# Softplus' sums on TensorE, rows copied out of PSUM at once, the norm in finer steps, the gate's product on GpSimd

## The chip, the cores and the metric

The kernel runs on one core of a Trainium2 chip. The metric is the device time of one execution in microseconds (us). The core has five engines that run side by side, each through its own list of instructions, in order: TensorE (PE in the profile, its weight loads PEld), VectorE (DVE), ScalarE (ACT), GpSimd (POOL) and SyncE (SP), which here only issues DMAs. They wait for each other through semaphores. SBUF is the working memory; PSUM, eight banks of 128 x 512 fp32 values, takes TensorE's results.

## The reference

The program is a network of four layers on an image of 2 x 256 x 32 x 32. The change lies in layer 0: a group norm, and then two Mamba blocks one after the other, each followed by a layer norm and a residual add. A block, for each of 2 x 1024 tokens with 256 channels and 512 inner channels:

```
xs, res = split(x @ in_w + in_b)
xs = silu(conv4(xs) + conv_b)               # causal, depthwise, 4 taps
dt, B, C = split(xs @ xproj_w)              # 16, 16, 16
delta = softplus(dt @ dt_w + dt_b)
h_t = exp(delta_t * A) * h_(t-1) + delta_t * B_t * xs_t     # 16 states for each channel
y = sum over states of h_t * C_t, + xs * D
out = (y * silu(res)) @ out_w + out_b
x = x + layernorm(out)
```

Layer 1 is a convolution attention over 7 x 7 taps, layers 2 and 3 are attentions with mixtures of experts. The reference computes in fp32.

## The kernel before

**Chunks and slots.** Layer 0 treats its 2048 tokens in chunks of 512. Two blocks of four chunks make eight units, numbered 0 to 7, and their scans follow each other. A tile holds 128 inner channels by 512 tokens, and there are four (dc = 0 to 3). `scan` (L415 on) runs over 16 states n and in each over the four tiles: 64 slots. A slot holds one Exp on ScalarE into PSUM (`m_da`, L468; three banks), one scan on VectorE (`m_h`, L472), one step of the readout of the previous state, and one step of whatever else is paced beside the scan. The right side of the scan, du times B, is made by GpSimd for two tiles at a time (L461), into six buffers, so three states. The readout (`rest`) has four steps for each state: four transposes by TensorE into a bank (`m_ht`, L440; three banks), and a multiply-add by VectorE into `m_ya` (L449), in states 0 and 10 a product by ScalarE.

**What is paced beside it.** `paced` (L552) hands out the steps of several generators over a range of slots. During the scan of a unit these are: `back` of the unit before (gate, product, output projection, norm, residual); `front` of the unit after (input projection, convolution, dt, softplus); weight loads; and `aside`, which folds the weights of layer 1's convolution into taps. The first 9 steps (`GATED`) of `back` lie in slots 0 to 35, its other 7 in slots 40 to 61; the first 22 steps (`HEAD`) of `front` in slots 0 to 38, its other 16, which are softplus', in slots 38 to 62; `aside` in slots 40 to 63. Projections, sums and tap transposes share two banks, `ps_mm`.

**Softplus** is max(z, 0) + log(1 + exp(-|z|)), with a correction for what is lost in rounding 1 + e. ScalarE leaves max(z, 0) in `delta`, exp(-|z|) in `e` and its logarithm in `ln` (the Exp and Ln of four tiles are one instruction each). Then w = (1 + e) - 1 is made, and GpSimd computes e - w (L405), adds it to `ln` (L407), adds that to `delta` (L409), and multiplies delta by `xs` into `du` (L411). The front of unit 0 runs ahead of all scans, with nothing beside it (`alone`), and there VectorE does this work.

**back.** The gate is projected and put through Silu; `m_y` gathers skip and readout by matmuls in a bank, and VectorE multiplies it by the gate (L516). Four output projections go into two banks and stay there; `norm_rows` takes mean and variance of all four from PSUM by VectorE, and ScalarE writes the normalised rows to SBUF (L168). After transposes (L179) and ScalarE's scale and bias (L540), GpSimd adds the result to x, in the second block also the input that is loaded again (L543, L548). The back of unit 7 runs after the last scan, interleaved by `both` with the convolution of image 0 (`early_acc`, 56 steps): one step of `back` after each three of its own.

**Order.** The order on each engine is that in which the built program lists its instructions. It follows the steps above, but the scheduler of the build moves instructions off their places in the source, so the built lists of both kernels were compared, engine by engine.

Of the kernel before, what the change touches and what calls it, by code (L numbers as in the profile page):

```python
# [10 lines left out]
F32 = mybir.dt.float32  # L11
# [8 lines left out]
P = 128  # L20
# [4 lines left out]
C = 256  # L25
# [208 lines left out]
class Mamba:  # L234
# [1 line left out]


    ASIDE = 10
    GATED = 9
    HEAD = 22  # L240

    def __init__(self, net, m, pools, xt, x, in_w, out_w, xproj_w, dt_w):
# [50 lines left out]
    def front(self, j, alone=False):  # L293
# [104 lines left out]
        for dc in range(NDC):  # L398
            w = du[:, dc, :]
            if alone:  # L400
                nc.vector.tensor_scalar(w, e[:, dc, :], 1.0, -1.0, ALU.add, ALU.add)
            else:
                nc.scalar.activation(w, e[:, dc, :], AF.Identity, bias=net.one)
                nc.scalar.activation(w, w, AF.Identity, bias=net.minus_one)
            eng.tensor_sub(w, e[:, dc, :], w)  # L405
            yield
            eng.tensor_add(ln[:, dc, :], ln[:, dc, :], w)  # L407
            yield
            eng.tensor_add(delta[:, dc, :], delta[:, dc, :], ln[:, dc, :])  # L409
            yield  # L410
            eng.tensor_mul(w, delta[:, dc, :], xs[:, dc, :])  # L411
            yield
        self.chunks[j] = xs, bd, ct, delta, du

# [67 lines left out]
            pass  # L482
        return before

    def back(self, j):

        net, nc, m, xt = self.net, self.net.nc, self.m, self.xt
        y, *sums = self.chunks.pop(j)
        tok = slice(j * TC, (j + 1) * TC)
        gate = self.one.tile([P, NDC, TC], F32, tag="gate", name=f"{m}_gate_{j}")  # L490
        for dc in range(NDC):
            ps = self.ps_mm.tile([P, TC], F32, tag="mm", name=f"{m}_g_{j}_{dc}")
            for kc in range(NCC):
                nc.tensor.matmul(
                    ps, lhsT=self.gate_sb[:, kc, dc * P : (dc + 1) * P], rhs=xt[:, kc, tok],
                    start=(kc == 0), stop=(kc == NCC - 1),
                )
            nc.scalar.activation(  # L498
                gate[:, dc, :], ps, AF.Identity, bias=net.col(f"{m}_in_b", NDC + dc)
            )  # L500
            yield
        nc.scalar.activation(gate, gate, AF.Silu)
        yield

        for dc in range(NDC):
            ps = self.ps_mm.tile([P, TC], F32, tag="mm", name=f"{m}_y_{j}_{dc}")
            nc.tensor.matmul(
                ps, lhsT=self.skip[:, dc, :], rhs=y[:, dc, :], start=True, stop=False
            )
            for k, ya in enumerate(sums):  # L510
                for i in range(TPC):
                    nc.tensor.matmul(
                        ps[:, i * P : (i + 1) * P], lhsT=ya[:, i, dc * P : (dc + 1) * P],
                        rhs=net.ident, start=False, stop=(k == 1 and i == TPC - 1),
                    )
            nc.vector.tensor_mul(y[:, dc, :], ps, gate[:, dc, :])  # L516
            yield
        o = self.one.tile([P, TPC, C], F32, tag="o", name=f"{m}_o_{j}")
        found = []
        for i in range(TPC):  # L520
            if i % 2 == 0:
                ps = self.ps_mm.tile([P, TC], F32, tag="mm", name=f"{m}_out_{j}_{i}")
            a = ps[:, i % 2 * C : (i % 2 + 1) * C]
            nc.tensor.matmul(
                a, lhsT=net.ones_row, rhs=self.out_b, start=True, stop=False
            )
            for dc in range(NDC):
                nc.tensor.matmul(  # L528
                    a, lhsT=y[:, dc, i * P : (i + 1) * P], rhs=self.out_sb[:, dc, :],
                    start=False, stop=(dc == NDC - 1),  # L530
                )
            found.append(a)
            yield
        tiles = [o[:, i, :] for i in range(TPC)]
        net.norm_rows(tiles, found, nc.scalar)
        yield
        for cc in range(NCC):
            ps = net.transposed(self.ps_mm, tiles, cc, "mm")
            r = self.one.tile([P, TC], F32, tag="r", name=f"{m}_r_{j}_{cc}", bufs=3)
            nc.scalar.activation(  # L540
                r, ps, AF.Identity, scale=net.col(f"{m}_ln_w", cc), bias=net.col(f"{m}_ln_b", cc)
            )
            nc.gpsimd.tensor_add(xt[:, cc, tok], xt[:, cc, tok], r)  # L543
            if self.x is not None:
                x = self.one.tile([P, TC], F32, tag="r", name=f"{m}_x_{j}_{cc}", bufs=3)
                at = j % (HW // TC) * TC
                nc.sync.dma_start(x, self.x[j // (HW // TC), cc, :, at : at + TC])
                nc.gpsimd.tensor_add(xt[:, cc, tok], xt[:, cc, tok], x)  # L548
            yield
# [25 lines left out]
def layer0(net, x, x_dram, m1, m2, load_image, taps, conv_dram, lg):  # L575
# [5 lines left out]
    with (  # L581
# [32 lines left out]
        for u, (m, j) in enumerate(units):  # L614
# [9 lines left out]
            rest = m.load_rest() if u and j == 0 else iter(())  # L624
            steps += [(f, Mamba.HEAD, 0, 38) for f in fronts]
            steps += [(rest, 1, 37, 38)]
            steps += [(f, 16, 38, 62) for f in fronts] + [(b, 7, 40, 61) for b in done]
            steps += [(rest, 1, 62, 63)]
            if u + 1 < len(units):
                n = 9 if u else 12  # L630
# [18 lines left out]
                acc = {0: taps.bank(ps_acc.tile([P, TC], F32, tag="acc", name="early_acc"))}  # L649
                steps += [(taps.convolve(0, pair, acc), 56, 3, 63)]  # L650
            before = m.scan(j, before, paced(63, steps), u == 0)
            done = [m.back(j)]
        taps.read(acc, lg)
        for _ in before:
            pass
# [1087 lines left out]
```

## Time and profile before

| | us |
|---|---|
| median of three runs | 2186.85 |
| range of the runs | 2185.29 to 2189.43 |
| profiled execution, its own time | 2188.29 |
| span of its profile | 2186.6 |
| busy: TensorE, its weight loads | 1894.0, 1335.5 |
| busy: VectorE, GpSimd, ScalarE | 1400.3, 1028.9, 959.2 |
| first scan, last scan's end | 53.26, 1031.3 |
| convolution of image 0 in the tail | 1034.6 to 1110.2 |

The span runs from the first instruction to the last; the profiled execution's time is 1.7 us longer. A line of the profile names the source line (L472), the engine, the operation and the tiles as `out<-in`; a count, busy us and mean ns of one follow, and then for how long the engine sat idle before such instructions and who released it. TensorE's counts are passes: a matmul of fp32 data is listed as two, a transpose as one. A busy TensorE is not TensorE at its peak, since a pass is listed from its start to its end and passes overlap. Line numbers up to L397 are the same in both kernels.

### The profile page before, as it was taken

The page shows a single profiled execution, that of the slowest core. Times are in us where ns is not written, and L with a number is a line of the kernel's source. Part 1 is how long each engine was busy: PE and PEld are TensorE (multiplying, and loading weights), DVE is VectorE, ACT ScalarE, POOL GpSimd, SP SyncE. Part 2 cuts the span into 40 slices and gives each one's busy share as a digit, 9 for nine tenths or more (in the row PEclk, how much of TensorE's full clock was granted, in tenths as well). Part 3 has the DMA queues.
Part 4 walks back from the last instruction along what each step waited for, and adds up shares of the span by engine and source line. Part 5 has one row for each costly group of instructions (what it writes and reads, how often), then busy time and mean ns, then how long its engine had stood idle before and what let it go on. Part 6 is the DMA issues. An engine that isn't in the chain of part 4 may idle for free.

```text
span 2186.6 us, 27311 instructions
## 1 busy us (share of the span) xinstructions
PE 1894.0 (87%) x9652; PEld 1335.5 (61%) x9652; DVE 1400.3 (64%) x2210; ACT 959.2 (44%) x1610; POOL 1028.9 (47%) x726
## 2 busy tenths in 40 slices
PE   6888898898978888788999989949999599859996
PEld 2464555556555655454646556539999467649995
DVE  6999998999999999899005475752222544432223
ACT  4676677767777767645013454411111132301111
POOL 3796787959698686965025420012332000023331
PEclk9869889898989889899999999969999799979997
DMA  2121121111212111310030100028998200059997
GB/s 106 45 68 39 37 69 35 58 35 45 62 47 60 38 49 35 85 42 17 0 64 1 48 15 10 20 82 306 326 329 323 82 10 10 20 206 327 329 323 292
DMA packets 90499, 223.87 MB, mean 102 GB/s; under 512 B 35467, under 2 KB 51728, under 8 KB 79732
## 3 DMA queue, kind: packets, MB, share of 16 engines
q1 hardware_dynamic: 77636, 198.29, 27.1%
q0 software_dynamic: 7728, 19.15, 2.9%
q10 hardware_dynamic: 4992, 4.59, 0.7%
q8 instruction: 81, 1.33, 0.3%
q14 instruction: 62, 0.51, 0.1%
HBM read 204.60 MB, written 19.37 MB: 102 GB/s over the span
## 4 chain that ended last, share of the span: by engine, by line
PE 32%; DVE 22%; issue 19%; POOL 11%; ACT 10%; DMA 5%; POOLq 0%; SPq 0%; DVEq 0%; ACTq 0%
DVE m_h L472 11%; DVE m_ya L449 6%; PE acc L762 3%; POOL x L1520 3%; POOL l_yd L1570 3%; PE m_ht L440 3%; PE early_acc L762 3%; PE av L1276 3%; ACT m_da L468 2%; PE sc L1250 2%; DMA l_yd<-y,target 2%; POOL m_h L461 2%; PE h L1099 2%; PE m_xd_ps L351 1%; PE w L1108 1%
## 5 line engine op out<-in xcount | busy, mean ns | idle before, releaser
L461 POOL TENSOR_TENSOR m_h<-m_du,m_b 128x1024 f32<-128x1024 f32 x254 | 594.5, 2364 | 196.0 <-PE m_ht L440 95.8
L440 PE MATMUL m_ht<-ident,m_h 128*128 128x128 f32 x2048 | 361.2, 305 | 119.4 <-DVE m_ya L449 83.9
L440 PEld LDWEIGHTS m_ht<-ident,m_h 128*128 128x128 f32 x2048 | 259.5, 154 | 317.8 <-DVE m_ya L449 112.7
L468 ACT ACTIVATE m_da<-m_delta,m_aneg 128x512 f32<-128x512 f32 x512 | 349.5, 690 | 220.8 <-DVE m_h L472 220.1
L1520 POOL DMA_INDIRECT x<-l_zd,source x82 | 84.8, 1034 | 573.1 <-DVE source L1465 217.1
L449 DVE SCALAR_TENSOR_TENSOR m_ya<-m_ht,m_ct,m_ya 128x512 f32<-128x512 f32 x448 | 320.2, 733 | 18.4 <-PE m_ht L440 17.5
L472 DVE TENSOR_TENSOR_SCAN m_h<-m_da,m_state,m_h 128x512 f32<-128x512 f32 x256 | 318.7, 1271 | 14.7 <-POOL m_h L461 8.7
L472 DVE TENSOR_TENSOR_SCAN m_h<-m_da,m_h 128x512 f32<-128x512 f32 x256 | 303.3, 1210 | 23.6 <-ACT m_da L468 13.1
L1550 PEld LDWEIGHTS h<-xts,we 128*128 128x128 f32 x2528 | 298.4, 194 | 7.1 <-issue 3.4
L1550 PE MATMUL h<-xts,we 128*128 128x128 f32 x2528 | 299.4, 277 | 2.2 <-issue 1.7
L1557 DVE TENSOR_TENSOR hid<-hid,h 128x512 f32<-128x512 f32 x79 | 54.3, 688 | 258.9 <-PE h L1550 258.9
L1556 ACT ACTIVATE hid<-h 128x512 f32<-128x512 f32 x79 | 47.2, 598 | 384.6 <-issue 324.0
L1564 PE MATMUL o<-we,hid 128*128 128x256 f32 x632 | 150.4, 380 | 2.2 <-DVE y L1569 1.6
L1570 POOL DMA_INDIRECT l_yd<-y,target x79 | 79.3, 1003 | 142.6 <-DVE y L1569 136.3
L1564 PEld LDWEIGHTS o<-we,hid 128*128 128x128 f32 x632 | 113.7, 190 | 15.7 <-DVE y L1569 2.8
L336 PE MATMUL m_conv<-m_pre,m_taps 128*128 128x512 f32 x240 | 114.6, 596 | 6.7 <-ACT m_gate L498 5.6
L762 PE MATMUL early_acc<-x,early 128*98 128x448 f32 (+21 forms) x308 | 97.0, 447 | 0.0
L762 PE MATMUL acc<-x,pair 128*98 128x416 f32 (+21 forms) x308 | 93.6, 452 | 0.0
L1569 DVE COPY y<-o 128x256 f32<-128x256 f32 x79 | 33.6, 425 | 69.6 <-PE o L1564 69.6
L309 PE MATMUL m_in<-x,m_in_sb 128*128 128x512 f32 x128 | 68.8, 663 | 9.8 <-ACT m_pre L313 6.9
L762 PEld LDWEIGHTS acc<-x,pair 128*98 128x98 f32 x308 | 47.7, 167 | 39.9 <-issue 34.5
L528 PE MATMUL m_out<-m_out_sb,m_xs 128*128 128x256 f32 x256 | 68.7, 397 | 0.0
(318 smaller groups left out, 2843.3 us busy)
## 6 DMA issues: line engine op xcount, KB each, us to landing
we<-in_l_experts_dram SPq DMA_DIRECT2D x82, 1536.0 KB
m_b<-m_bd SPq DMA_DIRECT2D x128, 256.0 KB
w<-in_l_w_dram SPq DMA_DIRECT2D x21, 256.0 KB
l_zd<-l_z SPq DMA_DIRECT2D x7, 512.0 KB
l_yl<-l_yd SPq DMA_DIRECT2D x10, 256.0 KB
l_yl<-l_yd ACTq DMA_DIRECT2D x10, 256.0 KB
early<-taps SPq DMA_DIRECT2D x7, 343.0 KB
pair<-taps SPq DMA_DIRECT2D x7, 343.0 KB
```

Source lines behind the costliest of these rows:

```text
L309: nc.tensor.matmul(ps, lhsT=self.in_sb[:, kc, mc * P : (mc + 1) * P], rhs=self.xt[:, kc, tok], start=(kc == 0), stop=(kc == NCC - 1),)
L336: nc.tensor.matmul(ps, lhsT=self.taps[:, dc * 4 + k, :], rhs=pre[:, dc, k : k + TC], start=(k == 0), stop=(k == 3),)
L440: nc.tensor.transpose(ps[:, dc * P : (dc + 1) * P], hs[dc // G][:, dc % G, i * P : (i + 1) * P], net.ident,)
L449: nc.vector.scalar_tensor_tensor(ya[:, i, :], ps, c, ya[:, i, :], ALU.mult, ALU.add)
L461: (nc.vector if start and n == 0 else nc.gpsimd).tensor_mul(h, du[:, g * G : (g + 1) * G, :], b.unsqueeze(1).to_broadcast(half))
L468: nc.scalar.activation(da, delta[:, dc, :], AF.Exp, scale=self.aneg[:, i : i + 1])
L472: nc.vector.tensor_tensor_scan(h, da, h, 0.0 if first else state[:, n, dc : dc + 1], ALU.mult, ALU.add)
L762: nc.tensor.matmul(a[:, lo - 16 * k : hi - 16 * k, co : co + n], lhsT=lhsT, rhs=self.x[:, kc, b, lo - r0 : hi - r0, ci : ci + n], start=(u ...
L1520: nc.gpsimd.indirect_dma_start(out=x, out_offset=None, in_=zd[:, :], in_offset=bass.IndirectOffsetOnAxis(ap=source[:, g : g + 1], axis=0), ...
L1550: nc.tensor.matmul(ps[:, at], lhsT=w12[:, s, kc, at], rhs=xt[:, kc * P : (kc + 1) * P], start=(kc == 0), stop=(kc == NCC - 1),)
L1564: nc.tensor.matmul(ps[:, :C], lhsT=ht[:, mc * P : (mc + 1) * P], rhs=w[:, 8 + mc, :], start=(mc == 0), stop=(mc == NHC - 1),)
L1570: nc.gpsimd.indirect_dma_start(out=yd[g], out_offset=bass.IndirectOffsetOnAxis(ap=target[:, g : g + 1], axis=0), in_=y, in_offset=None, bo ...
```

## The change

Softplus' e - w and the two adds leave GpSimd. ScalarE now makes w = 1 - (1 + e), TensorE adds delta + e + ln + w in a bank by four matmuls with the identity, ScalarE copies the sum to `delta`, and GpSimd keeps the product with `xs`. In the front of unit 0 (`alone`) VectorE still makes e - w, TensorE adds three terms, and VectorE multiplies straight from PSUM. Softplus takes 12 steps in place of 16, paced over slots 38 to 54.

In `back`, except for unit 7's, ScalarE copies `m_y` out of PSUM and GpSimd multiplies it by the gate, a tile later; the step for the last product makes `GATED` 10. ScalarE copies each pair of output projections to SBUF at once; statistics are taken from SBUF, row tile by row tile, in the following steps, and the normalising is split in two. That makes 10 steps after the gated ones in place of 7, paced over slots 38 to 62 in place of 40 to 61.

```diff
-    GATED = 9
+    GATED = 10
...
             if alone:
                 nc.vector.tensor_scalar(w, e[:, dc, :], 1.0, -1.0, ALU.add, ALU.add)
+                nc.vector.tensor_sub(w, e[:, dc, :], w)
             else:
                 nc.scalar.activation(w, e[:, dc, :], AF.Identity, bias=net.one)
-                nc.scalar.activation(w, w, AF.Identity, bias=net.minus_one)
-            eng.tensor_sub(w, e[:, dc, :], w)
-            yield
-            eng.tensor_add(ln[:, dc, :], ln[:, dc, :], w)
-            yield
-            eng.tensor_add(delta[:, dc, :], delta[:, dc, :], ln[:, dc, :])
-            yield
-            eng.tensor_mul(w, delta[:, dc, :], xs[:, dc, :])
+                nc.scalar.activation(w, w, AF.Identity, scale=-1.0, bias=net.one)
+            yield
+
+            pool, tag = (self.ps_ht, "ht") if alone and dc % 2 else (self.ps_mm, "mm")
+            ps = pool.tile([P, TC], F32, tag=tag, name=f"{m}_sp_{j}_{dc}")
+            parts = (delta, ln, du) if alone else (delta, e, ln, du)
+            for k, a in enumerate(parts):
+                nc.tensor.matmul(
+                    ps, lhsT=net.ident, rhs=a[:, dc, :], start=(k == 0), stop=(k == len(parts) - 1)
+                )
+            nc.scalar.copy(delta[:, dc, :], ps)
+            yield
+            eng.tensor_mul(w, ps if alone else delta[:, dc, :], xs[:, dc, :])
             yield
...
-            nc.vector.tensor_mul(y[:, dc, :], ps, gate[:, dc, :])
-            yield
+            if alone:
+                nc.vector.tensor_mul(y[:, dc, :], ps, gate[:, dc, :])
+            else:
+                nc.scalar.copy(y[:, dc, :], ps)
+                if dc:
+                    nc.gpsimd.tensor_mul(y[:, dc - 1, :], y[:, dc - 1, :], gate[:, dc - 1, :])
+            yield
+        if not alone:
+            nc.gpsimd.tensor_mul(y[:, dc, :], y[:, dc, :], gate[:, dc, :])
+        yield
         o = self.one.tile([P, TPC, C], F32, tag="o", name=f"{m}_o_{j}")
...
-            found.append(a)
-            yield
-        tiles = [o[:, i, :] for i in range(TPC)]
-        net.norm_rows(tiles, found, nc.scalar)
+
+            if i % 2:
+                nc.scalar.copy(
+                    o[:, i - 1 : i + 1, :], ps.rearrange("p (i c) -> p i c", c=C)
+                )
+            if i > 1:
+                stats(i - 2)
+            yield
+        stats(2)
         yield
+        stats(3)
+        rs = net.small.tile([P, TPC], F32, tag="ln_rs", name="ln_rs")
+        net.rstd(rs, mv[:, :, 1])
+        off = net.small.tile([P, TPC], F32, tag="ln_off", name="ln_off")
+        nc.vector.scalar_tensor_tensor(off, mv[:, :, 0], -1.0, rs, ALU.mult, ALU.mult)
+        yield
+        for i, a in enumerate(tiles):
+            nc.scalar.activation(
+                a, a, AF.Identity, scale=rs[:, i : i + 1], bias=off[:, i : i + 1]
+            )
+            if i % 2:
+                yield
...
-            steps += [(f, 16, 38, 62) for f in fronts] + [(b, 7, 40, 61) for b in done]
+            steps += [(f, 12, 38, 54) for f in fronts] + [(b, 10, 38, 62) for b in done]
...
-            done = [m.back(j)]
+            done = [m.back(j, u + 1 == len(units))]
```

More of the change, by code (lines that the diff above doesn't have):

```diff
@@ L483, in scan, with back @@
         return before
-    def back(self, j):
+    def back(self, j, alone=False):
         net, nc, m, xt = self.net, self.net.nc, self.m, self.xt
@@ L515, in back, with stats @@
                     )
-            nc.vector.tensor_mul(y[:, dc, :], ps, gate[:, dc, :])
+            if alone:
[4 more added lines that the diff above has]
+                    nc.gpsimd.tensor_mul(y[:, dc - 1, :], y[:, dc - 1, :], gate[:, dc - 1, :])
             yield
+        if not alone:
+            nc.gpsimd.tensor_mul(y[:, dc, :], y[:, dc, :], gate[:, dc, :])
+        yield
         o = self.one.tile([P, TPC, C], F32, tag="o", name=f"{m}_o_{j}")
-        found = []
+        tiles = [o[:, i, :] for i in range(TPC)]
+        mv = net.small.tile([P, TPC, 2], F32, tag="ln_mv", name="ln_mv")
+        def stats(i):
+            st = net.small.tile([P, 6], F32, tag="ln_st", name="ln_st")
+            nc.vector.bn_stats(out=st, in_=tiles[i])
+            nc.vector.bn_aggr(out=mv[:, i, :], in_=st)
         for i in range(TPC):
```

## The prediction

> **What bounds the kernel now.** I first read the share of each engine in every stretch of 100 us (columns: stretch, its length, busy us of PE, PEld, DVE, ACT, POOL, then TensorE's clock, DMA share, GB/s). The change lies in the stage from 53 to 1117 us.
>
> ```profile
> 400.00:500.00 100.00, 92.11 (x425) 59.46 (x425) 93.96 (x104) 70.15 (x107) 72.74 (x39) 0.88 0.14 45
> 600.00:700.00 100.00, 84.66 (x411) 55.61 (x410) 95.06 (x111) 76.08 (x128) 88.12 (x53) 0.91 0.18 55
> 1000.00:1100.00 100.00, 95.31 (x412) 56.77 (x413) 40.97 (x68) 27.73 (x40) 18.19 (x15) 1.00 0.04 10
> ```
>
> VectorE, busy 91 to 96 us in each 100, sets the pace of the scans; in the tail after them it is TensorE. Next, who VectorE waited for from 50 to 1035 us (total, times, longest):
>
> ```profile
> DVE m_h L472 <- POOL m_h L461: 19.2, 13, 4.9
> DVE m_h L472 <- ACT m_da L468: 19.0, 23, 2.5
> DVE m_ya L449 <- PE m_ht L440: 17.5, 26, 2.2
> DVE m_xs L516 <- PE m_y L512: 1.9, 3, 1.3
> ```
>
> Its idle time there, 57.6 us, is the most that better timing can return. Three groups that the change touches, from 100 to 1000 us (count, busy us, mean ns, idle time before):
>
> ```profile
> L409 POOL TENSOR_TENSOR m_delta<-m_delta,m_ln 128x512 f32<-128x512 f32 x28 | 35.6, 1271 | 1.5
> ...
> L516 DVE TENSOR_TENSOR m_xs<-m_y,m_gate 128x512 f32<-128x512 f32 x28 | 18.9, 674 | 1.9 <-PE m_y L512 1.9
> ...
> L702 ACT COPY w1ts<-w1t 128x512 f32<-128x512 f32 x21 | 12.3, 584 | 4.5 <-PE w1t L700 4.1 <-ACT m_state L432 0.2
> ```
>
> The scans begin a chunk at 543.22, 664.37, 789.13 us, so a chunk takes some 124 us and one of its 64 slots 1.95. I cut chunk 5 at its slots 0, 16, 32, 40, 48, 56 and 64 (same columns):
>
> ```profile
> 722.00:742.00 20.00, 19.53 (x85) 13.50 (x84) 17.96 (x22) 12.55 (x18) 11.26 (x6) 0.74 0.13 28
> 742.00:757.20 15.20, 13.58 (x85) 10.93 (x84) 14.19 (x18) 14.70 (x21) 15.04 (x9) 1.00 0.26 69
> 757.20:771.40 14.20, 8.21 (x38) 5.31 (x36) 14.20 (x20) 8.92 (x14) 14.04 (x9) 0.78 0.05 18
> 771.40:789.10 17.70, 15.16 (x77) 12.07 (x78) 15.61 (x20) 12.07 (x22) 17.39 (x14) 0.70 0.13 35
> ```
>
> From slot 40 on GpSimd is never idle (46.47 of 47.1 us): twelve softplus sums fall there, and the scans wait for its products at the chunk's end. TensorE has 10 us of idle time in it, 6 of them in slots 48 to 56, at a low clock.
>
> **The Trainium skill.** *GPSIMD Engine Reference*, section 1, gives GpSimd no access to PSUM: hence the new copies by ScalarE ahead of the gate's product. *VectorE: DVE Perf Modes*, section "The TRN2 errata", gives a ScalarE read from PSUM (172+N)/1.2 ns, for N = 512 an estimate of 570; the trace has 584, which I use. *TensorE: Matmul & The Clock Gate*, "Architectural detail", says that ScalarE, VectorE and GpSimd are strictly first in, first out, so a waiting copy holds all behind it; agreeing, ScalarE's Exp stands behind each eviction. Its Part 1 lets the clock fall when the array has been idle: four transposes take 0.66 us in the busy stretch at 757.50, 1.11 in the sparse one at 767.04.
>
> **The change, part by part**, against the profiled execution's 2188.29 us (span 2186.6, 1.7 around it). The runs' median is 1.44 lower, so I take the same difference from 2186.85.
>
> 1. *Gate's product.* Seven of eight chunks lose four VectorE products. The mean is 674 ns; from start to start (480.49 to 481.07) one holds VectorE about 0.60: 28 x 0.60 = -17 us on the bounding engine. The statistics now read SBUF: 416 ns on `t` in SBUF, 418 on `m_out` in PSUM, so nothing. ScalarE gets 28 copies of 584 ns, 16 us, covered by its 25 to 30% idle time; without cover, as much again. GpSimd gets 28 products of 1.27, 2.5 us per pair, in slots 18 to 36, where it idles (16.84 of 33 us busy in slots 16 to 32, by the same answer).
>
> 2. *Softplus.* GpSimd loses 84 operations (sub and two adds, 1.18 to 1.27 us): 104 us, 14.9 a chunk, all from slots 38 to 62. Priced from the built order with the rows' durations, it falls from 98 to 88 us a chunk with the four gate products, and that order leaves 5 to 8 us of GpSimd work in every four slots there (before: 10 to 12), against VectorE's 7.4. The 19.2 us wait should nearly go: -17 us. It was at the end of the chunk; what is late next there is TensorE.
>
> 3. *Softplus on TensorE.* Each of 28 tiles takes four matmuls of 128x512, two passes each. Passes follow each other after 0.43 us (four from 547.42 to 549.13): 4 x 2 x 0.43 = 3.44 us, 13.8 a chunk. Pricing the changed order in this way (transpose 0.11, projection step 0.43), TensorE has 31.9 us of work in slots 40 to 58, where VectorE has 30.8 (scan 1.19, `ya` 0.65 from start to start). Until now it had about 17. So it just fits, without its waits. What covers it: the order puts VectorE's `ya` later there, some 7 us behind the transposes that feed them. Without cover, 13.8 - 7 = 7 us a chunk.
>
> 4. *Copies and waits.* ScalarE gets 28 copies of `delta` and 14 of the projections, 584 ns: 25 us. The copy waits for the four matmuls; behind it on ScalarE stands the next Exp, for which a scan waits. The matmuls wait for ScalarE's two Identity steps; behind them on TensorE stand transposes, and behind these GpSimd, which needs the `h` buffers freed. The two `mm` banks alternate among sums, projections and tap transposes, each needing the eviction of the one before the last. Following chunk 5 step by step from slot 36: Exp and Ln with their table loads keep ScalarE 16.9 us between two stretches of Exp (slots 36 to 43: VectorE 16.0, a lead of three scans), 2 us of wait, as before roughly 1; from the first sum to the first scan of n = 11, 1.5 us; the products of n = 13 wait for the second sum, 1 to 2 us. So 2 us a chunk more than the same slots lose today: +14 us. Bounds: 0 (a denser, faster TensorE absorbs it, and holding banks for a shorter time pays) and +7 a chunk (step 3).
>
> 5. *Start.* From Ln (43.34 us) to the first scan (53.26) VectorE does all the sums. They go to TensorE, 3 x 0.86 = 2.6 us a tile, waiting from 43.3: tile 1 is ready at 48.5, tile 2 at 51.1. The product of h takes 1.22, the first scan can start at about 51.8: -1.5 us (0 to -3).
>
> 6. *Tail.* The last back has 20 steps instead of 16, the convolution beside it 56 steps at 3 each: 18 fit. The built order accordingly puts the last 8 transposes behind the convolution's last matmul, formerly 28 matmuls ahead. Before, this came at its end:
>
> ```profile
> 1105.02 1.27 POOL L548 TENSOR_TENSOR x<-x,m_x 128x512 f32<-128x512 f32 x1
> ...
> 1110.26 0.68 POOL L737 MEMSET pair<- 128x686 f32 x1 [2.59 <-PE early_acc L762]
> ```
>
> The second convolution (`acc`) began at 1116.57, 6.4 us after the first ended at 1110.2. Now: transposes 0.5, `r` 0.78, four GpSimd adds of 1.27 with the second x load (held by the first add's buffer) and memsets to about 8.5, then 4.5 pairs of `xs` copies and transposes at 0.9: 12.7 us, less the 0.9 us of transposes no longer inside: +5 us. Bounds +2 to +8. Other loads on SP keep their place apart from a few tap loads among the `b` loads; none ended a long wait before.
>
> Sum: -17 - 17 + 14 - 1.5 + 5 = -16.5 us, hence 2170.
>
> **Rivals.** *TensorE becomes the bound.* Place: slots 40 to 58 of seven chunks; price 7 us each. For: the work nearly doubles there, and TensorE is idle for only 0.5 us in the 20 before slot 40. Against: its low clock and the late `ya`. Then -17 - 17 + 49 - 1.5 + 5 = +18.5: 2205. It decides from (16.5 + 14) / 7 = 4.4 us of new waiting a chunk. *Everything new is hidden*, and early-freed banks take half of the 17.5 us for which VectorE waited on transposes: -17 - 19 - 9 + 2 - 1.5 + 5 = -40: 2147. *The cover was worthless*: GpSimd's products wait for later transposes instead, the 17 us do not return, the rest holds: 2187.
>
> **Chances.** Forecast 0.50, everything hidden 0.18, TensorE the bound 0.21, GpSimd's wait only replaced 0.11. No more than 0.2% (4.4 us) can be told from no change. Faster: 0.48 of the forecast, 0.18, and 0.03 of the last, 0.69. Slower: 0.20 and 0.02, 0.22. The rest, 0.09, is same. The likeliest case alone spans 2158 to 2182 (new waits of 0.3 to 3.7 us a chunk); the range reaches to the centres of the two outer rivals, leaving out half of each: 2145 to 2204.
>
> **What would show it.** Step 1: no gate product on VectorE, its busy time about 17 us lower. Step 2: `m_h` waiting for POOL below 5 us; POOL about 69 us less busy. Steps 3 and 4: TensorE busy above 90% in slots 40 to 58 at a clock near 1, and VectorE's waits for `m_da` and `m_ht` up by 14 us together; above 31 us the prediction falls. Chunks of 120 to 121 us. Step 5: first scan near 51.8. Step 6: `acc` about 11 to 12 us behind the last `early_acc`.

## The result

The changed kernel takes 2199.46 us (median of five runs, 2195.33 to 2200.05); the kernel before, run beside it five times, takes 2185.29. The ratio is 1.0059 with a 95% interval of 1.0045 to 1.0072: slower by 10 to 16 us, where 16.5 us less were forecast. The profiled execution has a span of 2198.3 us, 11.7 more than before. That span is the sum to explain.

### The profile page after: what moved, and what is told of

The parts are those of the page before. It is cut to its first block, busy times and chain, and to the rows that moved or that the text cites. A ratio compares the mean times of both kernels' runs of the same rounds, so it can differ in the third digit from the quotient of the medians.

```text
span 2198.3 us, 27827 instructions
## 1 busy us (share of the span) xinstructions
PE 1958.4 (89%) x9900; PEld 1359.3 (62%) x9900; DVE 1380.7 (63%) x2174; ACT 996.2 (45%) x1686; POOL 959.0 (44%) x670
## 4 chain that ended last, share of the span: by engine, by line
PE 24%; issue 14%; DVE 8%; POOL 8%; DMA 4%; ACT 2%; POOLq 0%; ACTq 0%; DVEq 0%
POOL x L1558 3%; PE acc L800 3%; POOL l_yd L1608 3%; PE av L1314 3%; PE sc L1288 2%; PE early_acc L800 2%; DMA l_yd<-y,target 2%; PE h L1137 2%; DVE m_h L478 2%; DVE m_ya L455 2%; PE w L1146 1%; DMA x<-l_zd,source 1%; POOL band L937 1%; PE l_g L1359 1%; DMA l_yl<-l_yd 1%
## 5 line engine op out<-in xcount | busy, mean ns | idle before, releaser
L446 PEld LDWEIGHTS m_ht<-ident,m_h 128*128 128x128 f32 x2048 | 251.1, 150 | 265.3 <-issue 105.9
L446 PE MATMUL m_ht<-ident,m_h 128*128 128x128 f32 x2048 | 330.0, 293 | 72.4 <-DVE m_ya L455 48.6
L549 PE MATMUL m_out<-m_out_sb,m_xs 128*128 128x256 f32 x256 | 73.1, 428 | 0.0
```

Of the source, the lines that this page charges most:

```text
L446: nc.tensor.transpose(ps[:, dc * P : (dc + 1) * P], hs[dc // G][:, dc % G, i * P : (i + 1) * P], net.ident,)
L549: nc.tensor.matmul(a, lhsT=y[:, dc, i * P : (i + 1) * P], rhs=self.out_sb[:, dc, :], start=False, stop=(dc == NDC - 1),)
```

## The profile after

The shares of the engines in the same three stretches of 100 us as before (columns: stretch, its length, busy us of PE, PEld, DVE, ACT, POOL, TensorE's clock, DMA share, GB/s):

```profile
400.00:500.00 100.00, 90.21 (x431) 54.93 (x430) 92.29 (x103) 72.87 (x111) 71.64 (x37) 0.94 0.16 47
600.00:700.00 100.00, 94.03 (x430) 59.34 (x429) 89.09 (x104) 74.50 (x132) 73.08 (x40) 0.91 0.21 56
1000.00:1100.00 100.00, 93.92 (x412) 56.49 (x410) 46.02 (x63) 30.14 (x43) 23.57 (x12) 1.00 0.01 4
```

TensorE is now as busy as VectorE, from 600 to 700 us more so. Over the whole span VectorE is busy for 1380.7 us (19.6 less), GpSimd for 959.0 (69.9 less). The work left the engines as it was meant to.

Who VectorE waited for from 50 to 1060 us (total, times, longest):

```profile
DVE m_ya L455 <- PE m_ht L446: 44.6, 37, 3.4
DVE m_h L478 <- POOL m_h L467: 23.4, 18, 7.6
DVE m_h L478 <- ACT m_da L474: 13.3, 22, 1.6
```

Before, from 50 to 1035 us, these were 17.5, 19.2 and 19.0. The wait for GpSimd, which should nearly have gone, is longer, and the wait for the readout's transposes is 27 us longer. VectorE lost 19.6 us of work and waits more than that.

Where it waits is told by cutting each unit at its scans. I worked this out from the trace (starts of the scans, busy time of VectorE between them); units 1 to 6, which have both a `front` and a `back` beside them, are averaged:

| us in a chunk (mean of units 1 to 6) | before | after |
|---|---|---|
| length | 124.7 | 126.0 |
| VectorE's work | 116.0 | 114.0 |
| VectorE idle in slots 0 to 24 | 1.0 | 0.6 |
| idle in slots 24 to 38 | 2.7 | 7.9 |
| idle in slots 38 to 58 | 2.3 | 3.5 |
| idle in slots 58 to 64 | 2.8 | 0.0 |

The span cut into its parts: first scan at 51.04 for 53.26, -2.2; unit 0 takes 118.1 for 112.1, +6.0; units 1 to 6, +7.5; unit 7, which has no `front` beside it, 113.0 for 117.6, -4.6; from the last scan to the span's end, +5.2. Together +11.9, against 11.7 between the spans; parts of one span add up whatever the cause, so this tells places, not causes. The first two together are +3.8.

Two stretches of unit 5 show it, slots 24 to 38 and slots 38 to 58 (same columns as above). First the kernel before:

```profile
703.70:733.40 29.70, 26.46 (x130) 16.75 (x129) 27.95 (x32) 17.74 (x24) 14.49 (x7) 0.84 0.17 36
733.40:775.90 42.50, 33.29 (x169) 24.48 (x169) 39.74 (x52) 34.03 (x48) 37.04 (x22) 0.82 0.14 38
```

And the kernel after:

```profile
713.90:748.40 34.50, 30.61 (x149) 18.70 (x148) 28.21 (x33) 23.24 (x33) 21.93 (x12) 0.90 0.12 32
748.40:786.40 38.00, 37.16 (x164) 25.24 (x165) 34.34 (x45) 32.86 (x51) 24.11 (x12) 0.92 0.13 38
```

In slots 38 to 58, where the softplus sums went, TensorE is busy 37.16 of 38.00 us, and the stretch is even shorter than before. The loss is in slots 24 to 38, ahead of any softplus sum: 4.8 us longer with the same work of VectorE (28.21 and 27.95 us).

What holds that stretch is told by VectorE's waits in it, summed over units 1 to 6 from the trace: for the transposes of the readout 27.9 us (before 8.9), for GpSimd's products of `h` 19.4 us (before 6.1). Behind them stand two waits of other engines. GpSimd from 50 to 1060 us:

```profile
POOL m_xs L527 <- ACT m_xs L525: 50.1, 18, 7.0
```

Its gate products stand at the head of its list until ScalarE has copied `m_y`, with the products of `h` behind them. This wait is new. And TensorE waits longer in front of the projection that needs Silu, with the transposes behind it, after and before:

```profile
PE m_xd_ps L351 <- ACT m_xs L345: 14.3, 6, 2.7
```

```profile
PE m_xd_ps L351 <- ACT m_xs L345: 4.2, 5, 1.4
```

The tail is as forecast. On the chain of work that ended last (start, length, what), the transposes follow the convolution, and the second input load waits for its buffer:

```profile
1118.15 0.47 PE mm_t L179 x4
...
1120.84 2.48 DMA m_x<-in_x_dram
```

`acc` began at 1130.41, 12.3 us behind the last `early_acc`, formerly 6.4.

## Experiments

Two theories stood at first. **A**: the gate's part makes the loss, because GpSimd's list stands behind ScalarE's copies. **B**: softplus' sums on TensorE make it.

### Each part alone

`soft_only` is the kernel before with

```diff
+            parts = (delta, ln, du) if alone else (delta, e, ln, du)
+            for k, a in enumerate(parts):
+                nc.tensor.matmul(
+                    ps, lhsT=net.ident, rhs=a[:, dc, :], start=(k == 0), stop=(k == len(parts) - 1)
+                )
+            nc.scalar.copy(delta[:, dc, :], ps)
...
-            steps += [(f, 16, 38, 62) for f in fronts] + [(b, 7, 40, 61) for b in done]
+            steps += [(f, 12, 38, 54) for f in fronts] + [(b, 7, 40, 61) for b in done]
```

> The kernel before with softplus' part alone (sums by TensorE, 12 steps in slots 38 to 54). Theory A, the gate's part makes the loss (ScalarE's copies of y hold GpSimd's list in slots 18 to 38): this one is then faster than before, GpSimd's wait at the chunk's end (19.2 us for VectorE) mostly goes and little replaces it, 2170 to 2180 us, and slots 24 to 38 keep the idle time of before. Theory B, TensorE's sums in slots 38 to 58 make it: 2190 us or more, VectorE's waits for m_da and m_ht there up by 10 us or more.

Measured: 2212.0 us, ratio 1.0119 (1.0102 to 1.0136).

`gate_only` is the kernel before with

```diff
-    GATED = 9
+    GATED = 10
...
-            nc.vector.tensor_mul(y[:, dc, :], ps, gate[:, dc, :])
+                nc.scalar.copy(y[:, dc, :], ps)
+                if dc:
+                    nc.gpsimd.tensor_mul(y[:, dc - 1, :], y[:, dc - 1, :], gate[:, dc - 1, :])
```

> The kernel before with the gate's part alone (y copied by ScalarE, product by GpSimd, 10 gated steps). Theory A: VectorE loses 17 us of work and waits as much or more, in slots 24 to 38 for the readout's transposes and at the chunk's end for GpSimd, which has 4 products more and still all sums; 2190 to 2205 us. Theory B: the gate's part by itself keeps its 17 us less the fuller GpSimd: 2170 to 2178 us.

Measured: 2199.46 us, ratio 1.0064 (1.0046 to 1.0082).

`norm_only` is the kernel before with

```diff
-        net.norm_rows(tiles, found, nc.scalar)
+            if i % 2:
+                nc.scalar.copy(
+                    o[:, i - 1 : i + 1, :], ps.rearrange("p (i c) -> p i c", c=C)
+                )
+            if i > 1:
+                stats(i - 2)
...
-            steps += [(f, 16, 38, 62) for f in fronts] + [(b, 7, 40, 61) for b in done]
+            steps += [(f, 16, 38, 62) for f in fronts] + [(b, 10, 38, 62) for b in done]
```

> The kernel before with the projected rows copied at once and the finer norm alone (10 steps in slots 38 to 62). All theories: during the scans within 3 us of before (the copies lie on ScalarE with its idle time, the banks come free sooner); in the tail the last 8 transposes fall behind the convolution's last matmul, acc begins about 12 us behind the last early_acc in place of 6.4. Sum 2188 to 2194 us. If the tail's term is wrong, 2185.

Measured: 2193.34 us, ratio 1.0035 (1.0021 to 1.0048). `acc` begins 10.1 us behind the last `early_acc`.

`after_dve_gate` is the kernel after with

```diff
-    GATED = 10
+    GATED = 9
...
-                nc.scalar.copy(y[:, dc, :], ps)
-                if dc:
-                    nc.gpsimd.tensor_mul(y[:, dc - 1, :], y[:, dc - 1, :], gate[:, dc - 1, :])
+            nc.vector.tensor_mul(y[:, dc, :], ps, gate[:, dc, :])
```

> The kernel after with the gate's product back on VectorE, straight from PSUM, and 9 gated steps. Theory A: the waits of slots 24 to 38 go with it, GpSimd no longer stands behind ScalarE's copies; 17 us of VectorE's work return, some 20 to 25 us of waiting go: 2188 to 2196 us, faster than the kernel after. Theory B: the 17 us return and the waits stay: 2210 to 2216 us.

Measured: 2211.86 us, ratio 1.0118 (1.0100 to 1.0136).

Each part alone costs time (+27, +14, +8 us), but together they cost 14, not 49. So parts can't be added; where each one loses is seen from the places (us in a chunk, units 1 to 6, as above):

| | length | work | idle 0-24 | 24-38 | 38-58 | 58-64 | unit 0 |
|---|---|---|---|---|---|---|---|
| before | 124.7 | 116.0 | 1.0 | 2.7 | 2.3 | 2.8 | 112.1 |
| after | 126.0 | 114.0 | 0.6 | 7.9 | 3.5 | 0.0 | 118.1 |
| soft_only | 127.3 | 117.1 | 5.6 | 2.3 | 2.2 | 0.1 | 116.5 |
| gate_only | 127.2 | 113.9 | 1.6 | 7.8 | 1.5 | 2.4 | 112.2 |
| norm_only | 125.5 | 116.2 | 1.3 | 2.6 | 4.3 | 1.1 | 111.8 |
| after_dve_gate | 128.0 | 116.2 | 0.8 | 2.7 | 8.0 | 0.3 | 117.9 |

The loss in slots 24 to 38 comes and goes with the gate's part: theory A has the place right. It has the price wrong: taking the part out of the kernel after made that 12 us slower, because 8.0 us a chunk were then lost in slots 38 to 58. Theory B's number came true for `soft_only`, but not in the place that it named: the loss lies in slots 0 to 24 of the next unit, where VectorE waits for GpSimd (21.7 us in the six units) and for transposes (10.2), and GpSimd for the last copies of the sums (early in unit 4, its product waits 2.45 us for one). Both theories fall in part.

### The steps, without the work

The gate's part also paces its steps more closely: ten over 35 slots, 3.5 apart, where nine lay 3.9 apart. **Theory C** keeps to GpSimd behind the copies. **Theory D** says that the place of the steps is the cause: y is gathered ahead of TensorE's wait for Silu, so the transposes come late behind it. `steps_only` is the kernel before with an empty step:

```diff
-    GATED = 9
+    GATED = 10
...
             nc.vector.tensor_mul(y[:, dc, :], ps, gate[:, dc, :])
             yield
+        yield
```

> The kernel before with an empty tenth gated step and nothing else: the gate's product stays on VectorE, only its steps lie 3.5 slots apart in place of 3.9. Theory C (GpSimd's list stands behind ScalarE's copies of y): no copies, so nothing new, 2183 to 2189 us. Theory D (the finer steps move the gathering of y ahead of TensorE's wait for Silu, so the readout's transposes come late behind it): the waits of slots 28 to 37 appear here too, about 5 us a chunk, 2205 to 2220 us with VectorE's product kept, 2195 at least.

Measured: 2199.41 us, ratio 1.0057 (1.0044 to 1.0071), with all work left where it was. Its slots 24 to 38 and 38 to 58 in unit 5:

```profile
709.60:746.70 37.10, 33.48 (x149) 19.75 (x147) 30.74 (x36) 21.44 (x29) 15.93 (x8) 0.82 0.13 30
746.70:783.80 37.10, 27.68 (x140) 19.37 (x140) 36.29 (x47) 30.20 (x44) 36.47 (x23) 0.82 0.15 42
```

The first stretch is longer than in the kernel after, while GpSimd and ScalarE have nothing new in it. VectorE has 2.5 us more work in it; its idle time is the same, 6.4 and 6.3 us. TensorE's wait for Silu is there as well:

```profile
PE m_xd_ps L351 <- ACT m_xs L345: 14.5, 6, 2.7
```

It is 14.3 us in the kernel after, 14.4 in `gate_only`, and 4.2 in `soft_only`, `norm_only` and `after_dve_gate`, as before. The steps shift where y is gathered in TensorE's list: in unit 5 the four gatherings begin at slots 21.2, 25.8, 29.8 and 31.8, before at 24.0, 29.6, 31.8 and 35.8. One round of it in unit 5, TensorE's wait for Silu, the transposes behind the projection, and VectorE's wait for these:

```profile
719.55 3.50 PE L351 MATMUL m_xd_ps<-m_xs,m_xp_sb 128*48 128x512 f32 x4 [2.53 <-ACT m_xs L345]
722.98 1.09 PE L440 MATMUL m_ht<-ident,m_h 128*128 128x128 f32 x8
...
723.68 1.41 DVE L449 SCALAR_TENSOR_TENSOR m_ya<-m_ht,m_ct,m_ya 128x512 f32<-128x512 f32 x2 [2.49 <-PE m_ht L440]
```

In slots 24 to 38 of units 1 to 6 VectorE then idles 5.8 us a chunk instead of 2.7. Theory D is shown for the kernel before. Moving the product to GpSimd on top of it (`gate_only`, 2199.46) changed nothing in the time: 2.0 us a chunk of VectorE's work became as much waiting in the same stretch. That waiting is theory C's. VectorE's waits in slots 24 to 38, us in units 1 to 6 together:

| | for transposes | for GpSimd's products of `h` |
|---|---|---|
| before | 8.9 | 6.1 |
| steps_only | 28.3 | 6.7 |
| copy_dve_product | 18.6 | 5.3 |
| gate_only | 26.0 | 20.8 |
| after | 27.9 | 19.4 |

The close steps bring the first column, and the products on GpSimd the second. So of the 31 us that the kernel after loses in this stretch, 19 are theory D's and 13 theory C's (less some 1 us of other waits that went).

`copy_dve_product` is `gate_only` with the product on VectorE, from the copy:

```diff
-                    nc.gpsimd.tensor_mul(y[:, dc - 1, :], y[:, dc - 1, :], gate[:, dc - 1, :])
+                    nc.vector.tensor_mul(y[:, dc - 1, :], y[:, dc - 1, :], gate[:, dc - 1, :])
```

> The kernel before with the gate's part, but the product made by VectorE from the SBUF copy: ScalarE's copies and the steps are as in gate_only, GpSimd has nothing of the gate. Theory C: without the products GpSimd no longer waits for copies, VectorE's waits for m_h from GpSimd in slots 28 to 38 fall to those of before (5 us in unit 2, little elsewhere), VectorE's work is that of before, 2185 to 2192 us. Theory D: the waits for transposes at slots 30 and 32 stay, about 4 us a chunk, and VectorE's 17 us are back, 2205 to 2217 us.

Measured: 2210.67 us, ratio 1.0112 (1.0094 to 1.0130). With nothing of the gate on GpSimd, slots 24 to 38 still lose 5.4 us a chunk; theory C alone would have them at 2.7. The wait for GpSimd did fall to that of before, as theory C had it; that for transposes stayed for the most part, and 8.3 us of waiting for ScalarE's copies came on top. The time lies 11 us above `steps_only`; it fits that the product from SBUF takes VectorE 1.15 us (mean of 28), from PSUM 0.68, 13 us in all (see the last section).

`after_tail2` is the kernel after with

```diff
-        both(taps.convolve(0, pair, acc), done[0], 3)
+        both(taps.convolve(0, pair, acc), done[0], 2)
```

> The kernel after with the last back interleaved after each two steps of the convolution in place of three, so that all its 20 steps fall inside. If the tail's term is right, acc begins 6 to 7 us behind the last early_acc in place of 12.3, and the time falls by 4 to 6 us, to 2193 to 2196. If something else sets that end (the adds and loads behind the scale and bias), 2199.

Measured: 2194.85 us, ratio 1.0034 (1.0020 to 1.0047): 5 us less by the ratios. `acc` begins 6.1 us behind the last `early_acc`. The tail's term is right.

`after_once` is `after_tail2` with

```diff
-                if dc:
-                    nc.gpsimd.tensor_mul(y[:, dc - 1, :], y[:, dc - 1, :], gate[:, dc - 1, :])
             yield
         if not alone:
-            nc.gpsimd.tensor_mul(y[:, dc, :], y[:, dc, :], gate[:, dc, :])
+            nc.gpsimd.tensor_mul(y, y, gate)
```

> As after_tail2, and the gate's product made by GpSimd in one instruction on all four tiles behind the last copy, in place of four that each wait for a copy. Theory C: GpSimd's products of h are no longer held behind the first three copies; VectorE's waits in slots 24 to 38 fall from 7.9 us a chunk to 3 to 5, 15 to 30 us below after_tail2, 2165 to 2180. Theory D: TensorE's order stays, and with it the waits at slots 30 and 32; within 5 us of after_tail2.

Measured: 2186.88 us, ratio 0.9998 (0.9989 to 1.0006), 8 us below `after_tail2`, so neither theory's number. Slots 24 to 38 keep 8.2 us of idle time (7.9 in `after_tail2`); the gain lies in slots 38 to 58 (2.0 for 3.5). Unit 0 is 2.7 us shorter in its trace, but its first scan began 2.0 us later. What lies behind the start of `acc` differs, too, 1070.2 for 1065.9 us, though no edit touches it: stages of single executions differ by several us.

### The steps put back

If the close steps are the cause, wide steps should free the kernel after. `after_39` changes one number in it:

```diff
-            steps = [(b, Mamba.GATED, 0, 35) for b in done]
+            steps = [(b, Mamba.GATED, 0, 39) for b in done]
```

> The kernel after with one number changed: its ten gated steps are paced over slots 0 to 39 in place of 0 to 35, which puts the gathering of y back where nine steps over 35 had it (3.9 slots apart). Theory D (the earlier gathering of y delays the readout's transposes around Silu): VectorE's idle time in slots 24 to 38 falls from 7.9 us a chunk to about 3, the other stretches stay, 25 to 30 us less, 2168 to 2176 us. Theory C (GpSimd's list stands behind ScalarE's copies): the four products still wait for their copies, within 5 us of 2199.

Measured: 2221.28 us, ratio 1.0166 (1.0147 to 1.0184). Slots 24 to 38 did fall to 4.3 us of idle time, but slots 38 to 58 rose from 3.5 to 10.1. In unit 5:

```profile
735.60:764.40 28.80, 25.83 (x140) 17.02 (x138) 26.15 (x29) 18.93 (x27) 18.20 (x10) 0.94 0.11 31
764.40:812.70 48.30, 42.00 (x181) 27.23 (x181) 37.81 (x48) 38.50 (x58) 28.59 (x15) 0.89 0.12 34
```

The first stretch is back at its length of before; the second is 10 us longer than in the kernel after. In this unit the last gathering begins at slot 35.8 in place of 31.8, as before the change. In slots 38 to 58 of units 1 to 6, VectorE's waits for GpSimd's products rose from 4.2 to 26.4 us and those for ScalarE's Exp from 5.9 to 15.1; those for transposes are nearly the same, 11.8 for 10.7. Why GpSimd is late there is not shown. Its last gate product waits for ScalarE's copy (14.4 us in these slots), but `after_dve_gate`, which has no such product, loses as much for GpSimd (26.5 us). Three more kernels have the wide steps.

`after_39_tail2` is `after_39` with

```diff
-        both(taps.convolve(0, pair, acc), done[0], 3)
+        both(taps.convolve(0, pair, acc), done[0], 2)
```

> As after_39, and the last back interleaved after each two steps of the convolution in place of three. If the two causes are apart, their gains add: 4 to 5 us below after_39.

Measured: 2212.00 us, ratio 1.0122 (1.0099 to 1.0146); the tail's gain adds, if anything, more than its 5 us.

`gate_39` is `gate_only` with

```diff
-            steps = [(b, Mamba.GATED, 0, 35) for b in done]
+            steps = [(b, Mamba.GATED, 0, 39) for b in done]
```

> The kernel before with the gate's part alone, its ten gated steps over slots 0 to 39. Theory D: it keeps VectorE's 17 us less work and loses the waits of gate_only, and pays only for a fuller GpSimd: 2170 to 2182 us. Theory C: as gate_only, 2195 to 2203 us.

Measured: 2195.15 us, ratio 1.0041 (1.0029 to 1.0052). Without the sums the wide steps gain some 5 us over `gate_only`, if anything (the two intervals touch), not 20, so the number is theory C's: idle time in slots 24 to 38 falls from 7.8 to 4.7, and rises from 1.5 to 4.1 in 38 to 58.

`once_39` makes the same edit, 39 for 35, in `after_once`.

> As after_39_tail2, with the gate's product in one GpSimd instruction behind the last copy. Theory C still in part: below after_39_tail2 by the waits for single copies, 5 us or more. Theory D alone: no better, and worse if 4.7 us of one instruction hold the products of h and the output projection: 0 to 10 us above after_39_tail2.

Measured: 2201.05 us, ratio 1.0075 (1.0054 to 1.0095): 10 us better than `after_39_tail2`, so the product in one instruction is better here, too. Theory D alone would have it no better.

### What the sums cost

`gate_norm` is the kernel before with the edits of `gate_only` and `norm_only`, which is all of the change but softplus' part:

```diff
-            steps += [(f, 16, 38, 62) for f in fronts] + [(b, 7, 40, 61) for b in done]
+            steps += [(f, 16, 38, 62) for f in fronts] + [(b, 10, 38, 62) for b in done]
```

> The kernel before with the gate's part and the finer norm, softplus' sums left on GpSimd: the kernel after less softplus' part. Theory E (TensorE's list is full from Silu to the chunk's end; the sums fit only where the gathering of y is done by slot 38, as ten steps over 35 slots have it): softplus' part costs little or gains on top of this one, 2199 to 2208 us here. If the sums cost here what they cost with y gathered later (18 to 26 us more): 2175 to 2182 us.

Measured: 2197.21 us, ratio 1.0065 (1.0045 to 1.0085), where the kernel after has 1.0059. In this company softplus' part is worth nothing that can be measured, though it costs 27 us on the kernel before, and 18 on `norm_only` (`after_dve_gate`, 1.0118 for 1.0035). Unit 5, slots 38 to 58 and 58 to 64:

```profile
739.60:779.40 39.80, 32.90 (x178) 25.38 (x178) 39.61 (x51) 35.06 (x55) 38.04 (x23) 0.83 0.15 44
779.40:788.50 9.10, 8.34 (x29) 5.21 (x30) 9.10 (x12) 5.24 (x8) 8.94 (x7) 0.62 0.19 63
```

GpSimd still makes all the sums (38.04 of 39.80 us busy), and yet VectorE hardly waits at the chunk's end: 0.5 us a chunk in units 1 to 6, before 2.8 (the profiled execution is the fastest of its runs, 2191.67 us). That wait goes without softplus' part, too; it goes with softplus' part alone as well (0.1 in `soft_only`).

`after_sum2` takes two matmuls out of each sum, which then lacks two terms; `after_sum8` doubles all four:

```diff
-            parts = (delta, ln, du) if alone else (delta, e, ln, du)
+            parts = (delta, ln, du) if alone else (ln, du)
```

```diff
-            parts = (delta, ln, du) if alone else (delta, e, ln, du)
+            parts = (delta, ln, du) if alone else (delta, e, ln, du, delta, e, ln, du)
```

> The kernel after with two matmuls in each of softplus' sums in place of four, those on ln and w; max(z, 0) and e are left out of the sum, all waits on ScalarE stay. TensorE has 2 x 4 x 2 x 0.43 = 6.9 us a chunk less. Theory E: TensorE sets the pace in slots 38 to 58, 4 to 7 us a chunk are gained, 2150 to 2172 us. If what the sums cost is their waits and their place in the lists: within 8 us of 2199.

Measured: 2205.07 us, ratio 1.0094 (1.0077 to 1.0112).

> The kernel after with each of the four matmuls of a sum made twice (the sum is doubled by it). TensorE has 13.8 us a chunk more. Theory E: nearly all of it is paid, 2270 to 2296 us. If TensorE had room: below 2240.

Measured: 2293.81 us, ratio 1.0499 (1.0478 to 1.0519). Slots 38 to 58 of unit 5 with two matmuls, and with eight:

```profile
750.20:791.00 40.80, 35.85 (x192) 25.79 (x191) 38.71 (x48) 36.14 (x58) 33.38 (x18) 0.95 0.19 50
```

```profile
814.20:866.90 52.70, 49.62 (x192) 30.86 (x193) 34.73 (x44) 34.76 (x53) 23.98 (x12) 0.94 0.08 27
```

Four more matmuls cost 94 us, nearly the 7 x 13.8 = 97 us of their passes. Two fewer gain nothing, the time is 6 us longer: TensorE gets 5 us of idle time in this stretch, and the stretch is no shorter (40.8 us for 38.0), with VectorE busy for 38.71 of it. Theory E, that TensorE's sums set the pace in the kernel after, falls. In the kernel after they just fit.

`once_three` starts from `after_once`, makes e - w on GpSimd and sums three terms:

```diff
-                nc.scalar.activation(w, w, AF.Identity, scale=-1.0, bias=net.one)
+                nc.scalar.activation(w, w, AF.Identity, bias=net.minus_one)
+                nc.gpsimd.tensor_sub(w, e[:, dc, :], w)
...
-            parts = (delta, ln, du) if alone else (delta, e, ln, du)
+            parts = (delta, ln, du)
```

> As after_once (the gate's product in one instruction, the last back after each two steps; 2187 us), with e - w made by GpSimd again and three matmuls in a sum. TensorE has 3.4 us a chunk less, GpSimd 5 us more, behind ScalarE's second step. Theory E: 1.5 to 3 us a chunk are gained, 2165 to 2177 us. If GpSimd's place behind ScalarE decides: 2187 or more.

Measured: 2200.43 us, ratio 1.0073 (1.0057 to 1.0090), slower than `after_once`: a chunk takes 126.4 for 124.7, and unit 0 ends 2.6 us later. That is the case in which GpSimd's place behind ScalarE decides, not theory E's.

### The steps moved forward

Theory F says that slots 24 to 38 lose because transposes, gathering and the projection behind Silu stand in a row in TensorE's list. `once_28` and `once_31` are `after_once` with

```diff
-            steps = [(b, Mamba.GATED, 0, 35) for b in done]
+            steps = [(b, Mamba.GATED, 0, 28) for b in done]
```

and 31 in place of 28.

> As after_once (2187 us with ten gated steps over slots 0 to 35), the steps over 0 to 28: all of y is gathered ahead of TensorE's first matmul behind Silu, and the last two gatherings fill its wait for Silu. Theory F (slots 24 to 38 lose because TensorE's list has transposes, gathering and the projection behind Silu in a row there, wherever they lie): VectorE's idle time in 24 to 38 falls from 8.2 us a chunk to 4 to 6, 2165 to 2178 us, below both kernels. If the stretch only hands its wait on, to slots 18 to 24 or 38 to 48: 2183 to 2195.

Measured: 2179.51 us, ratio 0.9965 (0.9951 to 0.9979): faster than the kernel before by 4.6 to 10.7 us, and so than the kernel after. Slots 24 to 38 and 38 to 58 of unit 5:

```profile
701.80:732.80 31.00, 29.22 (x131) 16.74 (x130) 28.09 (x31) 21.72 (x30) 23.93 (x10) 0.85 0.12 35
732.80:775.00 42.20, 39.58 (x195) 27.53 (x193) 38.33 (x48) 35.57 (x56) 26.13 (x15) 0.95 0.13 42
```

Idle time in slots 24 to 38 is 4.6 us a chunk (8.2 in `after_once`), in 38 to 58 it is 2.4, at the chunk's end 0.0; the chunk takes 122.7. The idle time is as theory F had it; the time lies between its range and that of the other reading. The profiled execution, at 2174.52 us, is faster than the median.

> As once_28, over slots 0 to 31: one gathering ahead of the convolution's last matmuls, one ahead of Silu's wait, one between the projection's halves. Theory F: between after_once and once_28, 2172 to 2183 us.

Measured: 2200.56 us, ratio 1.0063 (1.0043 to 1.0084), far above theory F's range. Slots 24 to 38 lose 8.8 us a chunk. Yet TensorE's wait in front of the projection has gone in both (2.8 us here, and 2.9 in `once_28`, there for a copy of y). So that wait marks the kernels with ten steps over 35 slots, but it is not by itself what the stretch loses. The trace shows where the 31 loses: at slot 31, 6.3 us a chunk, for 2.5 in `once_28`. There, in unit 5, the last gathering stands between the halves of the projection:

```profile
732.95 1.02 PE L513 MATMUL m_y<-m_xs,m_skip 128*128 128x512 f32 x2
...
736.46 4.52 POOL L528 TENSOR_TENSOR m_xs<-m_xs,m_gate 128x2048 f32<-128x2048 f32 x1 [6.73 <-ACT m_xs L525]
...
738.23 0.75 DVE L455 SCALAR_TENSOR_TENSOR m_ya<-m_ht,m_ct,m_ya 128x512 f32<-128x512 f32 x1 [3.49 <-PE m_ht L446]
...
743.32 1.28 DVE L478 TENSOR_TENSOR_SCAN m_h<-m_da,m_state,m_h 128x512 f32<-128x512 f32 x1 [2.72 <-POOL m_h L467]
```

VectorE waits first for the transposes behind it, then for a product of `h` that stands behind GpSimd's gate product, and this one waited for the last copy (such waits are 29.9 us in `once_31`, 9.3 in `once_28`). Both theories' waits meet in one slot; no run takes them apart there.

## Why the prediction was wrong

**Step 1, the gate's product: the step that failed.** VectorE's work fell about as priced, by 2.1 us in a chunk of units 1 to 6 and 19.6 us over the span. But the step left out the finer pacing, and so priced it at nothing, and it called ScalarE's copies and GpSimd's products covered by the two engines' idle time, GpSimd's in slots 18 to 36. `steps_only` shows that an empty tenth step alone costs 12.6 us, and `gate_only` that moving the product on top of it returns nothing. In the kernel after, slots 24 to 38 lose 5.2 us a chunk more than before, 31 us in six units, which stand nowhere in the sum: 19 us more of waiting for transposes, which the pacing brings, and 13 us more for products of `h`, which stand behind gate products and copies. The step counted idle time by engine; what was needed was the order in which TensorE, ScalarE and GpSimd hand this stretch to each other.

**Step 2, GpSimd's wait.** Right in its place: GpSimd is busy for 69.9 us less (69 forecast), and VectorE's idle time in slots 58 to 64 went from 2.8 to 0.0 us a chunk, 16 us for 17 forecast. Wrong in the total (23.4 us, not below 5), since GpSimd's products are late in slots 28 to 37 now. And the reason was not the only one: `gate_norm`, with all sums still on GpSimd, loses only 0.5 us there.

**Steps 3 and 4, the sums and their waits.** Right for TensorE: 97.8% busy in slots 38 to 58 of unit 5, and the sums just fit, as the passes of 0.43 us had it; `after_sum8` pays such passes nearly in full. The waits in slots 38 to 58 rose by 1.2 us a chunk in units 1 to 6, against 2 forecast. `m_da` and `m_ht` together rose by 21.4 us, between the 14 forecast and the 31 set as the limit, but mostly in slots 24 to 38, ahead of the sums, so that the number fits is luck. Missed was unit 0: with no `back` beside it, it still takes 6.0 us more (3.8 with the earlier first scan taken off), and `gate_norm` (111.6) shows that this is softplus' part.

**Steps 5 and 6.** First scan at 51.0 (51.8 forecast), `acc` 12.3 us behind the last `early_acc` (11 to 12); the tail cost 5.2 us where 5 were forecast, and `after_tail2` takes 5 of them back. The mechanism is right; the match to a fraction of a us is luck, since the stretch behind `acc` alone differs by some us between executions.

**The rivals.** The time lies between two of them. TensorE as the bound (2205) was close in time, and `after_sum2` speaks against its mechanism. The wait that is only replaced (2187) has the mechanism, GpSimd waiting for later transposes, but at 0.11 it got too little chance and too small a price: it took back step 2's 17 us alone, and left the gain of step 1 standing.

So the sum should have read, in the terms measured. In units 1 to 6: -12 of work, -16 at the chunk's end, +31 in slots 24 to 38, +7 in slots 38 to 58, -2 in slots 0 to 24; +6 in unit 0, -5 in unit 7, -2 at the start, +5 in the tail. That is +12, against 11.7 between the spans.

## What to carry to other kernels

Where several engines run in order beside a loop, moving steps by two to four slots can cost as much as the work that is saved beside them, so a change of pacing is a change to be priced, and to be tried alone with an empty step. An engine's idle time in a stretch is no cover unless the thing waiting for it is not itself waited for: follow one chunk's chain through every engine, and ask of each freed microsecond which wait takes it. Parts that each lose when alone can fit together and the other way round, so undo them in pairs before keeping or dropping one.

## What was not expected of the hardware

The cost of TensorE's work had a knee: in the same place of the same kernel, four more matmuls of 128x512 in each of 28 sums cost 94 us and two fewer saved none (2293.8, 2199.5 and 2205.1 us). Why two fewer saved none is not shown.

VectorE also stood still inside an instruction. The scalar_tensor_tensor of 128x4 that makes the norm's offset took from 0.42 us (mean of six in `gate_only`) to 1.70 us (mean of six in `soft_only`). The Trainium skill, *GPSIMD Engine Reference*, section 1, names VectorE instructions with two SBUF inputs as those that contend with GpSimd; this one has such inputs, and the traces agree. Over all twenty of them, 124 of these instructions begin while GpSimd is in the middle of one; 122 of the 124 end within 16 to 31 ns of the end of an instruction of GpSimd, however long that takes, and all others take 0.14 to 0.17 us. In the kernel before:

```profile
526.85 1.27 POOL L407 TENSOR_TENSOR m_ln<-m_ln,m_du 128x512 f32<-128x512 f32 x1
...
527.51 0.63 DVE L166 SCALAR_TENSOR_TENSOR ln_off<-ln_mv,ln_rs 128x4 f32<-128x4 f32 x1
```

It costs more where the instruction is large. In `copy_dve_product` VectorE multiplies two tiles in SBUF. The 11 of its 28 products that begin inside a GpSimd product of `h` end 546 to 549 ns after that one's end and take 1.2 to 2.8 us; the 15 that begin with GpSimd idle take 0.66 to 0.69 (the other two begin inside a GpSimd instruction of 0.6 us and take 0.66 and 0.79). In the kernel before the same product reads one tile from PSUM, and all 32 take 0.66 to 0.69, the seven that begin while GpSimd is busy too. Together this is 13 us of VectorE's time in `copy_dve_product`, so a product is not worth the same from SBUF as from PSUM. No kernel here was built to test it; that the ends coincide is what the traces show.
